# Preparation of the dense passes, kept places and the order of the plain pairs in a four-layer fp32 kernel

## The chip, the cores and the metric

The kernel runs on one core of a Trainium2 chip. A core has a matrix engine (TensorE, PE in the profile, with its weight loads as PEld), a vector engine (VectorE, DVE), an activation engine (ScalarE, ACT), a general engine (GpSimd, POOL) and a queue that issues all DMAs here (SyncE, SP). The metric is device time in microseconds; a kernel's time is the median of its runs. All arithmetic is in fp32, so each product on TensorE is recorded as two matmul instructions.

## The reference, cut to what matters

The input x is 2 x 1024 x 1024 (two batches of 1024 rows, 1024 columns). Four layers with a residual each follow one another:

```python
x = x + attn_a(layernorm(x))     # 32 heads of 32, causal, rotary, plus 10 adapter keys
x = x + ffn(layernorm(x))        # first dense pass
x = x + attn_b(layernorm(x))     # 8 heads of 16, not causal, with biases
x = x + ffn(layernorm(x))        # second dense pass, the same weights

def ffn(x):
    base = x @ W_base.T + b_base                       # 1024 x 1024
    weights = sparsemax(x @ W_router.T + b_router)     # over 8 experts
    h = einsum('bsd,edr->bser', x, lora_A)             # rank 16 each
    return base + einsum('bser,bse,ero->bso', h, weights, lora_B)
```

So a dense pass is, for each row, one large product, and a low-rank part: a hidden vector of 8 x 16 values, scaled by the router's weights, times lora_B.

## The kernel before

**Attention and filler.** `attend` runs an attention in rounds. In a round it issues the score products of one piece twice, in the two layouts (`st` at L394 for the output, `sc` at L322 for the row maximum), the exponential of `st` on ScalarE (`pt`, L506), the row minimum of the negated scores on VectorE (L335, into `part` and `nmax`), the exponential of those for the sums (`pr`, L343), and the output products (`y`, L416). Between the rounds, TensorE is given other work, the filler, by `fill.run`: so many estimated nanoseconds of it. For attention B that is 2650 a round in the first half and 1500 in the second (`FILL_B`). TensorE's order is written by hand this way, SP's too after attention A; VectorE, ScalarE and GpSimd get their order from the framework's scheduler, and every engine works through its order without overtaking.

**Filler as generators.** The filler is a queue of Python generators in `Filler`. A generator yields after each product a number of nanoseconds, or a mark. `WAIT` ends the round's filler. `AHEAD` makes the Filler call `prepare` on the next `Dense` in the queue, if its gate is open; one such call runs that generator to its next mark, and `READY` says that it is prepared. When a gate opens later, `fill.open` makes up for the calls missed. When a `Dense` that isn't ready comes to the front of the queue inside an attention, `step` prepares it once and gives the round no filler; outside (`cold`), it prepares it to the end and goes on at once. `fill.need` runs filler until a key is there.

From attention B on the queue is: first pass of batch 0 (`f1(0)`), projection of B for batch 0 (`project_b(0)`), `f1(1)`, `project_b(1)`, and then, behind gates, the second pass in four ranges of four 128-row tiles (`f2`), each opened by the output projection (`project_wo`) of the rows that it needs. Attention B of batch 0 starts behind `project_b(0)`, that of batch 1 behind `project_b(1)`.

**A dense pass** (`ffn`) works on pairs of tiles, the odd one first (`seq`). `fetch` loads a tile of x, `normalize` is the layer norm (L244 to L261) followed by the addition of the bias on GpSimd (L239), `turn` transposes the normalized tile on TensorE (L204, into a bank of PSUM, copied out by L232 or L234), `hidden` makes the low-rank hidden values and the router's logits (`hp`) and runs the router on VectorE (L1221 to L1243, which ends with the scaled hidden values `hs`), `turned` transposes these (`ht`) and copies them out on ScalarE (`hwT`, L1266). Ahead of the first pair a pass calls `fetch(0)` and `fetch(1)`, `normalize(0)` and `normalize(1)` in that order, with marks between them.

Most pairs use a scheme with seven products of half-size blocks instead of eight (`seven_added`), with sums of blocks as factors. It needs *places*: a ring for the summed weights, which `piece` loads from `tf` in DRAM, a work tile, and a third tile cut into a place for one x (`room["x"]`) and one transposed tile (`room["xt"]`). They are the tiles in which attention B keeps its q, k and v. `take_room` asks for them, in each `ffn` anew, so that each new set has to wait for the tile before it as a whole.

Two first pairs are done plainly (`plain`): that of the very first pass, where the summed weights are only being made, and that of the first second-pass range (`late_room`), where attention B still has the places. A plain pair is 2 tiles by 2 column halves (n) by 8 products `fo` of 128 x 512, each group closed by the low-rank product with `hwT` and by an addition on VectorE (L1318). In the first pass's pair n=0 goes wholly ahead of n=1, and `turned` comes right ahead of the first low-rank product, after eight products; in the `late_room` pair four products of n=0 come first, then n=1, then the rest of n=0, and `turned` comes after twelve.

PSUM banks: `bank` is one bank, shared by the output projection, the low-rank transpose and some others; `next_bank` goes back and forth between two, so that a bank comes back after one group.

**The projection of B** (`project_b`) goes tile by tile, t = 0 to 7: v (`bv`), then the transposes of the next tile, its layer norm two tiles ahead, then q and k (`bq`), which VectorE shuffles into two layouts (L1489 to L1494). It gives `AHEAD` at the head of tiles 6 and 7.

**The output projection** (`project_wo`) is called in the attention's `late` hook, one product `bo` a round. It loads x (`xo`), adds the bias on GpSimd, and starts with the round in which the attention's output `yT` is copied out by ScalarE (L1545).

The second-pass range of tiles 4 to 7 of batch 0 has a case of its own, `behind`:

```python
behind = (b, k, tiles[0]) == (0, 1, 4)
fetch(0)
if not behind:
    fetch(1)
...
if behind:
    fetch(1)
    yield WAIT
    yield WAIT
    normalize(1)
    yield WAIT
```

Of the kernel before, what the change touches and what calls it, by code (L numbers as in the profile page):

```python
# [14 lines left out]
F32 = mybir.dt.float32  # L15
# [5 lines left out]
P = 128  # L21
B, T, C = 2, 1024, 1024
NT = T // P
# [124 lines left out]
def tile_model(ctx: ExitStack, tc: tile.TileContext, d, out: bass.AP):  # L148
# [1025 lines left out]

    tf = {(i, c): dram.tile([P, HF], F32, name=f"tf{i}_{c}") for i in (2, 3, 4) for c in range(4)}

    def ffn(b, k, src, dst, w, wk, tiles, places, free=lambda: True, there=lambda t: True):


# [4 lines left out]

        seq = [t for p in range(0, len(tiles), 2) for t in (tiles[p + 1], tiles[p])]
        xs, xns, xts, hws, stores = {}, {}, {}, {}, deque()
        room = {}

        def fetch(i):
            t = seq[i]  # L1190
            xs[t] = room["x"] if room and i % 4 == 3 else wk.tile([P, C], F32, tag="x", name=f"xf{b}_{k}_{t}", bufs=3)
            sp.dma_start(xs[t], src(t))

        def normalize(i):
# [90 lines left out]

        def plain(p):
            order = [(n, c) for n in range(2) for c in range(NC)]
            if late_room:
                order = order[:4] + order[NC:] + order[4:NC]
            for i in range(2):  # L1290
                t = seq[2 * p + i]
                ops = {}
                for n, c in order:
                    cols = slice(n * HF, (n + 1) * HF)
                    if n not in ops:
                        ops[n] = next_bank([P, HF], f"fo_f{b}_{k}_{t}_{n}")
                    op = ops[n]
                    mm(op, lhsT=xts[t][:, c, :], rhs=w["wb"][:, c, cols], start=(c == 0), stop=False)
                    yield HF * COL
                    if late_room and (n, c) == (0, 3):  # L1300

                        pin_add(xs[t][:, HF:], op, xs[t][:, HF:])
                    if (i, n, c) == (0, 0, 3):
                        normalize(2)
                    if late_room and (i, n, c) == (1, 0, 1):
                        while stores:
                            sp.dma_start(*stores.popleft())
                        fetch(3)
                    if (i, n, c) == ((1, 1, 5) if late_room else (0, 1, 3)):
                        normalize(3)  # L1310
                    if i and c == 5:
                        yield from turn(2, (1 - n if late_room else n,))
                    if c < NC - 1:
                        continue
                    if (i, n) == (0, int(late_room)):
                        hwT = turned(p)
                    mm(op, lhsT=hwT[:, 1 - i], rhs=w["lb"][:, cols], start=False, stop=True)
                    dve.tensor_add(xs[t][:, cols], op, xs[t][:, cols])  # L1318
                    store(t, n)
                    yield HF * COL  # L1320
            yield from transposed(xns[seq[3]], place_xt(3), f"f{b}_{k}_{seq[3]}", by=(next_bank, next_bank))
            fill.flush("wb")
            if first:
                b11, b12 = (w["wb"][:, :4, n * HF : (n + 1) * HF] for n in range(2))
                for c in range(4):
                    fill.chore("wb1", lambda c=c: pin_sub(b12[:, c], b12[:, c], b11[:, c]))

        def take_room():
            ring, work, more = places()
            room.update(ring=ring, work=work, x=more[:, :2].rearrange("p a c -> p (a c)"),  # L1330
                        xt=more[:, 2:].rearrange("p a (b c) -> p (a b) c", c=P))
            if not first:
                for c in range(4):
                    piece(2, c)


        behind = (b, k, tiles[0]) == (0, 1, 4)
        fetch(0)
        if not behind:
            fetch(1)  # L1340
        yield None
        normalize(0)
        if not behind:
            yield None
            normalize(1)
        yield READY
        if not late_room:
            take_room()
        if behind:
            fetch(1)  # L1350
            yield WAIT
            yield WAIT
            normalize(1)
            yield WAIT
        for i in range(2):
            yield from turn(i, by=(bank, next_bank))
        n_pairs = len(tiles) // 2
# [77 lines left out]
    def project_b(b, w, fk, wk, st):  # L1435
        xs, ready = {}, {}

        def fetch(t):
            xs[t] = fk.tile([P, C], F32, tag="x", name=f"xb{b}_{t}", bufs=3)
            sp.dma_start(xs[t], x2[b, t])  # L1440

        def normalize(t):
            xn = layernorm(fk, "xn", xs.pop(t), f"b{b}_{t}", behind=True)
            ready[t] = xn, fk.tile([P, NC, P], F32, tag="xt", name=f"xt_b{b}_{t}", bufs=2)

        fetch(0)
        fetch(1)
        yield None
        normalize(0)
        yield READY  # L1450
        qk = st["qk", b] = wk.tile([P, 2, T], F32, tag=f"qkb{b}", name=f"qk{b}", bufs=1)
        kq = st["kq", b] = wk.tile([P, 2, T], F32, tag=f"kqb{b}", name=f"kq{b}", bufs=1)

        vm = st["vm", b] = wk.tile([P, NT, HB, 2 * EB], F32, tag=f"vm{b}", name=f"vm{b}", bufs=1)
        pool.memset(vm, 0.0)
        normalize(1)
        fetch(2)
        fetch(3)
        yield from transposed(*ready[0], f"b{b}_0", by=(bank, next_bank))
        for t in range(NT):  # L1460
            xnT = ready.pop(t)[1]
            if t >= NT - 2:
                yield AHEAD
            cols = slice(t * P, (t + 1) * P)
            vp = next_bank([P, P], f"bv{b}_{t}")
            for c in range(NC):
                mm(vp, lhsT=xnT[:, c, :], rhs=w["wv"][:, c, :], start=(c == 0), stop=(c == NC - 1))
                yield P * COL
            for s in range(2):
                hs, cs = slice(4 * s, 4 * s + 4), slice(s * EB, (s + 1) * EB)  # L1470
                o = slice(4 * s * EB, (4 * s + 4) * EB)
                dve.tensor_add(
                    vm[:, t, hs, cs], vp[:, o].rearrange("p (h e) -> p h e", e=EB),
                    w["b_v"][:, o].rearrange("p (h e) -> p h e", e=EB),
                )
            if t + 1 < NT:
                yield from transposed(*ready[t + 1], f"b{b}_{t + 1}", by=(bank, next_bank))
            if t + 2 < NT:
                normalize(t + 2)
            if t + 4 < NT:  # L1480
                fetch(t + 4)
            qp = next_bank([P, 2, P], f"bq{b}_{t}")
            for j in range(2):
                for c in range(NC):
                    mm(qp[:, j, :], lhsT=w["wqk"][:, c, j * P : (j + 1) * P], rhs=xnT[:, c, :],
                              start=(c == 0), stop=(c == NC - 1))
                    yield P * COL
            both = fk.tile([P, 2, P], F32, tag="both", name=f"both{b}_{t}", bufs=1)
            dve.tensor_add(both, qp, w["b_qk"][:, :, None].to_broadcast([P, 2, P]))  # L1489
            dve.tensor_scalar(qk[:, :, cols], both, low, None, ALU.mult)  # L1490
            for j in range(2):
                dve.stream_shuffle(kq[:, j, cols], both[:, j], [(i + EB) % (2 * EB) for i in range(2 * EB)])

            dve.tensor_scalar(kq[:, :, cols], kq[:, :, cols], low, after, ALU.mult, ALU.add)  # L1494
        yield ("bproj", b)

    def project_wo(b, n, yT, w, fk):
        xs = {}

        def fetch(i):  # L1500
            xs[i] = fk.tile([P, C], F32, tag="xo", name=f"xo{b}_{4 * n + i}", bufs=2)
            sp.dma_start(xs[i], x2[b, 4 * n + i])
            pool_add(xs[i], xs[i], w["b_o"])

        fetch(0)
        fetch(1)
        yield 0.0
        for i in range(4):
            t = 4 * n + i
            x = xs.pop(i)  # L1510
            for h in range(2):
                op = bank([P, HF], f"bo{b}_{t}_{h}")
                mm(op, lhsT=yT[:, i * P : (i + 1) * P], rhs=w["wo"][:, h * HF : (h + 1) * HF], start=True, stop=True)
                dve.tensor_add(x[:, h * HF : (h + 1) * HF], op, x[:, h * HF : (h + 1) * HF])
                if h == 0:
                    yield HF * COL
            sp.dma_start(x3[b, t], x)
            fill.done.add(("x3", b, t))
            if i == 1:
                fill.open(("wo", b, n))  # L1520
            if i + 2 < 4:
                fetch(i + 2)
            yield HF * COL
# [205 lines left out]
```

## Time and profile before

| | us |
|---|---|
| median of 3 runs (2460.93 to 2471.85) | 2467.08 |
| profiled execution, its own time | 2465.06 |
| its span | 2463.3 |
| PE busy | 2375.2 (96%) |
| DVE busy | 1433.7 (58%) |
| ACT busy | 1100.7 (45%) |
| POOL busy | 593.4 (24%) |
| mean granted clock of PE over the span | 0.988 |

Attention A, its projection and the first normalizations fill the span up to about 1461 us. Then come the first pass of batch 0 (to about 1605), the projection of B for batch 0 (to about 1659), attention B with the rest as filler (from 1671 to about 2298, with the projection of batch 1 ending at about 1969), and the last two second-pass ranges without an attention beside them.

A line of the timeline names its start, its length, engine, code line, operation, output and input by the program's names, shapes and count; in brackets stands how long the engine was idle ahead of it, and what released it. A list of waits gives the engine and line that waited, what for, the total, the number of times and the longest. The row "PEclk" and the last-but-two column of a table by stretches give the clock that TensorE was granted, 1.00 being full speed. A matmul row's end is modelled and lies about 0.2 us behind the start of the next matmul.

### The profile page before, as it was taken

The numbers are of one execution on the slowest core, as the hardware profiler recorded it, in microseconds if no ns is written. First come the engines' busy times: TensorE is split into PE (matmuls) and PEld (weight loads), VectorE is DVE, ScalarE is ACT, GpSimd is POOL, SyncE is SP. The second block draws the span as 40 slices with busy tenths as digits, with TensorE's granted clock in tenths as the row PEclk, the third lists the DMA queues.
The fourth block names the chain that finished last, engine by engine and source line by source line (L and its number), as shares of the span: only waits on it lengthen the run. The fifth ranks groups of instructions, "written<-read, shape, count | busy, mean of one in ns | idle before, by whom it ended". The sixth has DMA issues, their size and how long they took to land.

```text
span 2463.3 us, 60412 instructions
## 1 busy us (share of the span) xinstructions
PE 2375.2 (96%) x25063; PEld 1089.1 (44%) x25063; DVE 1433.7 (58%) x4310; ACT 1100.7 (45%) x2104; POOL 593.4 (24%) x927
## 2 busy tenths in 40 slices
PE   7999999999999999999999999999999989989999
PEld 4435444455344545444433444584334633223354
DVE  7676665666656666665631254476656756563444
ACT  2246665665665666656642000012454445654100
POOL 1332232232423322332211132202111102121332
PEclk9999999999999999999999999999999999989999
DMA  6633332323333333323212754432332202122443
GB/s 216 208 93 88 99 92 79 104 88 104 124 97 105 89 108 98 89 83 125 87 58 89 240 176 133 150 112 86 95 95 87 96 18 95 56 107 95 168 156 120
DMA packets 173043, 271.54 MB, mean 110 GB/s; under 512 B 16224, under 2 KB 76768, under 8 KB 172768
## 3 DMA queue, kind: packets, MB, share of 16 engines
q1 hardware_dynamic: 172768, 267.68, 33.8%
q8 instruction: 196, 3.21, 0.5%
q14 instruction: 79, 0.65, 0.1%
HBM read 212.05 MB, written 55.57 MB: 109 GB/s over the span
## 4 chain that ended last, share of the span: by engine, by line
PE 84%; DVE 8%; DMA 3%; ACT 2%; issue 1%; POOL 1%; SPq 1%; DVEq 0%; POOLq 0%
PE st L394 9%; PE sc L322 8%; PE y_A L416 5%; PE y L200 5%; PE z L200 3%; PE st L392 3%; PE y_f L198 3%; PE z_f L198 3%; PE x L200 3%; PE y_v L200 3%; PE y_f L200 2%; PE x_f L198 2%; PE y_B L416 2%; PE y_p L198 2%; DVE pr_A L335 2%; PE x_v L200 2%
## 5 line engine op out<-in xcount | busy, mean ns | idle before, releaser
L506 ACT ACTIVATE pt<-st 128x1024 f32<-128x1024 f32 (+1 forms) x418 | 426.0, 1019 | 617.9 <-PE st L394 483.6
L343 ACT ACTIVATE pr_A<-pr_A,nmax_A 128x896 f32<-128x896 f32 (+7 forms) x512 | 389.9, 765 | 53.3 <-DVE nmax_A L335 52.9
L335 DVE CUSTOM_DVE_ANT_0 pr_A<-sc,mask 128x512 f32<-128x512 f32 (+3 forms) x512 | 250.9, 537 | 193.7 <-PE st L394 99.4
L322 PE MATMUL sc<-kT,qT 32*128 32x512 f32 (+3 forms) x1536 | 326.3, 521 | 4.1 <-POOL qT L816 2.1
L394 PE MATMUL st<-qT,kT 32*128 32x512 f32 (+3 forms) x1536 | 306.2, 485 | 0.0
L335 DVE CUSTOM_DVE_ANT_0 pr_A<-sc,mask,part_A 128x512 f32<-128x512 f32 (+1 forms) x256 | 156.2, 647 | 146.6 <-PE sc L322 96.3
L401 POOL TENSOR_SCALAR_AFFINE_SELECT pt<-pt 128x256 f32<-128x256 f32 x256 | 105.2, 429 | 466.1 <-ACT pt L506 466.1
L343 ACT ACTIVATE pr_B<-pr_B,nmax_B 128x1024 f32<-128x1024 f32 x128 | 145.5, 1139 | 49.4 <-DVE nmax_B L335 49.3
L239 POOL TENSOR_TENSOR xf<-xf,b_base 128x256 f32<-128x256 f32 x100 | 73.1, 763 | 390.1 <-DVE xn_f L261 347.7
L416 PE MATMUL y_A<-pt,v 128*32 128x512 f32 (+3 forms) x1536 | 157.0, 496 | 0.0
L322 PE MATMUL sc<-kq,qk 32*128 32x512 f32 x512 | 147.3, 652 | 7.1 <-DVE nmax_B L335 4.8
L394 PE MATMUL st<-rows_B,kq 32*128 32x512 f32 x512 | 145.2, 643 | 6.4 <-ACT pt L506 6.0
L394 PEld LDWEIGHTS st<-qT,kT 32*128 32x128 f32 x1536 | 133.5, 185 | 16.4 <-issue 11.4
L392 PE MATMUL st<-rows_A,ones 3*128 3x512 bf16 (+3 forms) x768 | 127.6, 329 | 4.0 <-DVE nmax_A L335 3.5
L335 DVE CUSTOM_DVE_ANT_0 pr_B<-sc,zeros,part_B 128x512 f32<-128x512 f32 x128 | 90.9, 747 | 63.9 <-PE sc L322 63.9
L335 DVE CUSTOM_DVE_ANT_0 pr_B<-sc,zeros 128x512 f32<-128x512 f32 x128 | 83.4, 687 | 74.7 <-PE sc L322 74.7
L392 PEld LDWEIGHTS <-ones 3*128 3x128 bf16 x768 | 36.6, 91 | 193.3 <-issue 185.9
L322 PEld LDWEIGHTS sc<-kT,qT 32*128 32x128 f32 x1536 | 112.9, 184 | 18.0 <-issue 4.7
L815 POOL TENSOR_TENSOR qr<-qr,sin 128x256 f32<-128x256 f32 x64 | 60.5, 946 | 227.7 <-DVE qr L811 226.8
L343 ACT ACTIVATION_READ_ACCUMULATOR pr_A<-pr_A,nmax_A 128x1 f32 x512 | 97.1, 190 | 0.0
L200 PE MATMUL y<-tt,wqk 128*32 128x512 f32 x768 | 92.6, 594 | 0.0
L416 PEld LDWEIGHTS y_A<-pt,v 128*32 128x32 f32 x1536 | 33.6, 108 | 117.8 <-issue 108.0
(427 smaller groups left out, 4235.1 us busy)
## 6 DMA issues: line engine op xcount, KB each, us to landing
tt<-td SPq DMA_DIRECT2D x252, 256.0 KB, 2.8
qkb_f<-tf SPq DMA_DIRECT2D x84, 256.0 KB, 2.9
qkb_s<-tf SPq DMA_DIRECT2D x84, 256.0 KB, 3.1
wqk<-in_w_attnT SPq DMA_DIRECT2D x32, 512.0 KB, 5.1
xf<-x SPq DMA_DIRECT2D x25, 512.0 KB, 4.0
xa<-in_x SPq DMA_DIRECT2D x16, 512.0 KB, 6.0
wv<-in_w_attnT SPq DMA_DIRECT2D x8, 1024.0 KB, 5.4
yd<-ys SPq DMA_DIRECT2D x32, 256.0 KB, 2.5
```

Source lines behind the costliest of these rows:

```text
L198: return pe.matmul(out, lhsT=lhsT, rhs=rhs, start=start, stop=stop, skip_group_check=True)
L200: pe.matmul(out[i : i + 32], lhsT=lhsT[:, i : i + 32], rhs=rhs, start=start, stop=stop, skip_group_check=True)
L239: pool.tensor_add(dst[:, i : i + 2 * P], a[:, i : i + 2 * P], b[:, i : i + 2 * P])
L322: yield w * COL, lambda: pe.matmul(dst[:, o : o + w], lhsT=self.qt[rows, qc : qc + P], rhs=self.kt[rows, c0 : c0 + w], start=True, stop=True)
L335: minimum[0] = dve.tensor_tensor_reduce(pr[:, c0 : c0 + w], sc[:, i, o : o + w], m, -self.scale, BIG if c0 == 0 else self.part[:, col], AL ...
L343: tc.keep_in_program_order(act.activation(pr[:, :nk], pr[:, :nk], AF.Exp, bias=self.nmax[:, col], scale=-1.0, accum_out=self.sums[:, col]))
L392: yield w * COL / 4, lambda: pe.matmul(dst[:, o : o + w], lhsT=of["ones"][three, :], rhs=self.rows[three, off : off + w], start=True, stop ...
L394: yield w * COL, lambda: pe.matmul(dst[:, o : o + w], lhsT=self.kt[rows, kb * P : (kb + 1) * P], rhs=rhs, start=self.extra, stop=True)
L401: pool.affine_select(out=dg, in_=dg, compare_op=ALU.is_ge, fill=0.0, base=0, pattern=[[0, 2], [1, P]], channel_multiplier=-1)
L416: pe.matmul(self.y[32 * h : 32 * h + 32, off : off + w], lhsT=self.value(h, kb), rhs=pt[h // 2][:, h % 2, o : o + w], start=self.opens, st ...
L506: act.activation(pt[:, :, low_:wide_], st[:, :, low_:wide_], AF.Exp, scale=ts[0][0].scale)
L815: pool.tensor_mul(qr[:, hs], qr[:, hs], sin[:, cols][:, hs])
```

## The change

There are five edits, all in the order of the work; no product is added or left out.

1. `project_b` gives a third `AHEAD`, behind the v products of tile 6. The pass behind it is thereby prepared in three goes: both fetches at the head of tile 6, the first normalization behind tile 6's v, the second at the head of tile 7.
2. The places are kept in a dictionary outside `ffn`: one for each batch's first pass, and one for all four second-pass ranges. `take_room` asks for places only if none are there. In the second pass the tile that goes to `room["x"]` is now the range's second (i % 4 == 1), if the places are there already, instead of its fourth.
3. The case `behind` is gone; tiles 4 to 7 start like any other range.
4. Both plain pairs take the same order: four products of n=0, eight of n=1, four of n=0. `turned` comes after ten products, and the first low-rank product after twelve.
5. `project_wo` yields once more ahead of its first product, which so moves by one round.

```diff
+    kept = [{}, {}, {}]
+
     def ffn(b, k, src, dst, w, wk, tiles, places, ...):
-        room = {}
+        room = kept[2 if k else b]
         def fetch(i):
             t = seq[i]
-            xs[t] = room["x"] if room and i % 4 == 3 else wk.tile(...)
+            xs[t] = room["x"] if room and i % 4 == (1 if k else 3) else wk.tile(...)
         def plain(p):
             order = [(n, c) for n in range(2) for c in range(NC)]
-            if late_room:
-                order = order[:4] + order[NC:] + order[4:NC]
+            order = order[:4] + order[NC:] + order[4:NC]
...
                     if i and c == 5:
-                        yield from turn(2, (1 - n if late_room else n,))
+                        yield from turn(2, (1 - n,))
+                    if (i, n, c) == (0, 1, 5):
+                        hwT = turned(p)
                     if c < NC - 1:
                         continue
-                    if (i, n) == (0, int(late_room)):
-                        hwT = turned(p)
         def take_room():
-            ring, work, more = places()
-            room.update(...)
+            if not room:
+                ring, work, more = places()
+                room.update(...)
             if not first:
                 for c in range(4):
                     piece(2, c)
-        behind = (b, k, tiles[0]) == (0, 1, 4)
         fetch(0)
-        if not behind:
-            fetch(1)
+        fetch(1)
         yield None
         normalize(0)
-        if not behind:
-            yield None
-            normalize(1)
+        yield None
+        normalize(1)
         yield READY
         if not late_room:
             take_room()
-        if behind:
-            fetch(1)
-            yield WAIT
-            yield WAIT
-            normalize(1)
-            yield WAIT
...
     def project_b(...):
             if t >= NT - 2:
                 yield AHEAD
...
+            if t == NT - 2:
+                yield AHEAD
             if t + 1 < NT:
                 yield from transposed(...)
...
     def project_wo(...):
         fetch(0)
         fetch(1)
         yield 0.0
+        yield 0.0
```

## The prediction

> **What bounds the kernel now.** I read the page's first two parts, then TensorE's waits, its rows in order of time from 1450 us on (attention A, before that, is untouched), and the granted clock in short stretches.
>
> ```profile
> span 2463.3 us, 60412 instructions
> PE 2375.2 (96%) x25063; PEld 1089.1 (44%) x25063; DVE 1433.7 (58%) x4310; ACT 1100.7 (45%) x2104; POOL 593.4 (24%) x927
> PEclk9999999999999999999999999999999999989999
> ```
>
> TensorE is busy for 96%, so the kernel can win only what TensorE stands still (88 us in all), and what it runs at half clock. The waits (total, times, longest) name the few that this change touches:
>
> ```profile
> PE xt_f L204 <- DVE xn_f L261: 15.4, 3, 5.8
> PE st L394 <- ACT pt L506: 6.0, 10, 2.0
> PE ht_f L204 <- DVE hs_f L1243: 3.8, 3, 3.3
> PE bo L200 <- ACT yT L1545: 2.8, 4, 0.7
> PE fo_f L198 <- ACT hwT_f L1266: 2.7, 2, 2.3
> ```
>
> In order of time (start, length, what, in brackets the idle time before it):
>
> ```profile
> 1477.38 0.44 PE L204 MATMUL ht_f<-ident,hs_f 128*128 128x128 f32 x2 [3.29 <-DVE hs_f L1243]
> 1478.28 1.55 PE L198 MATMUL fo_f<-lb,hwT_f 128*128 128x512 f32 x2 [0.46 <-ACT hwT_f L1266]
> ...
> 1665.08 1.94 PE L204 MATMUL xt_f<-ident,xn_f 128*128 128x128 f32 x8 [5.83 <-DVE xn_f L261]
> ...
> 1974.66 1.94 PE L204 MATMUL xt_f<-ident,xn_f 128*128 128x128 f32 x8 [5.34 <-DVE xn_f L261]
> ...
> 2008.90 1.13 PE L198 MATMUL fo_f<-lb,hwT_f 128*128 128x512 f32 x2 [2.26 <-ACT hwT_f L1266]
> ...
> 2160.26 0.70 PE L394 MATMUL st<-rows_B,kq 32*128 32x512 f32 x2 [2.03 <-ACT pt L506]
> 2169.23 1.94 PE L204 MATMUL xt_f<-ident,xn_f 128*128 128x128 f32 x8 [4.19 <-DVE xn_f L261]
> ```
>
> These are six places: the first plain pair (1477), the start of the dense pass behind each projection of B (1665, 1974), the second plain pair (2009), the start of the second-pass range of tiles 4 to 7 (2150 to 2170), and the output projections (four waits of 0.70). A stall costs more than its length (stretch, its length, busy us of PE, PEld, DVE, ACT, POOL, then the granted clock and DMA):
>
> ```profile
> 1478.00:1480.00 2.00, 1.72 (x3) 0.93 (x4) 1.25 (x3) 0.23 (x1) 0.00 (x0) 0.71 0.72 262
> 1480.00:1482.00 2.00, 2.00 (x3) 0.67 (x2) 1.97 (x4) 0.00 (x0) 0.00 (x0) 0.50 0.36 132
> ...
> 1666.00:1668.00 2.00, 2.00 (x11) 2.00 (x10) 1.18 (x2) 0.59 (x1) 2.00 (x3) 0.50 0.02 4
> 1668.00:1670.00 2.00, 2.00 (x11) 2.00 (x11) 0.32 (x1) 0.00 (x0) 0.31 (x1) 0.50 0.03 8
> 1670.00:1672.00 2.00, 2.00 (x15) 1.41 (x14) 0.00 (x0) 0.00 (x0) 0.00 (x0) 1.00 0.00 0
> ```
>
> After the stall TensorE works at half clock for some 3.5 to 6 us, and loses half of that.
>
> **The change part by part.** No product is added or removed; all of it is order.
>
> *First plain pair.* Four products take 3.44 us (1510.21 to 1513.65), 0.86 each. The transpose of the low-rank input is now asked for after ten products, not eight: 1.72 us later. What it waits for, hs, ends at 1477.3 and stays there: in the built order one batch-norm statistic (0.68) of the earlier-called fourth normalization takes the place ahead of it of one weight sum (0.68), and its input landed at 1467.7 (issued 1463.0, 4.7 to land). So the stall goes from 3.29 to 1.57, and the copy hwT (0.37) lies beside two products: 0.46 gone. Half clock here cost (0.29+0.50+0.06) x 2 us = 1.70 (1482 to 1484 has 0.94). Against this the new order hands the bank of n=0 straight to the next tile: its first product waits for the addition L1318 (starts 0.04 after the matmul row's end, 0.69 long, release 0.17; the row's end is 0.2 after the next issue): 1.1 us, and the same behind the pair, where a wait of 0.42 stood: 0.7. 1.72+0.46+1.70-1.8 = **2.1** (0.4 if the clock still drops; 3.9 without the bank waits).
>
> *Third go behind the projections (1665 and 1974).* The second tile's normalization was called only when TensorE needed it:
>
> ```profile
> 1653.05 0.42 DVE L1489 TENSOR_TENSOR both<-bq,b_qk 128x256 f32<-128x256 f32 x1 [2.88 <-PE bq L198]
> ...
> 1660.87 0.68 DVE L244 BATCH_NORM_STATS2 stats_f<-xf 128x6 f32<-128x512 f32 x1
> ...
> 1664.12 0.81 DVE L261 TENSOR_SCALAR xn_f<-xf,mv_f,r_f 128x1024 f32<-128x1024 f32 x1
> ```
>
> It is two statistics, five tiny operations and L261: about 3.2 us of VectorE (0.68+0.63+0.20+0.13+0.27+0.15+0.21+0.81=3.1), two 0.20 activations, four GpSimd additions of 0.73, and, for the first pass, take_room's four DMAs on SP (already issued without a wait at 1641). Now the first tile's chain falls into VectorE's hole of 2.88 us before 1653, the second's behind the sixth tile's kq, ending by my count at 1657.9; wanted at 1659.25. Both inputs are there (fetched by 1641, 4 us to land), and the statistic of the third tile, which the order puts inside the chain, reads data issued at 1647.2 and 1957.3, early enough. What is late next: the copies out of the bank (0.24 us, as at the same transposes elsewhere), and GpSimd. Its additions now lie beside VectorE's work on the last qk. [...] I take 0.4 in the queue, 0.3 on TensorE. Gains: 5.83 + 0.5 x (1670.0-1665.1) = 8.3, less 0.3, **8.0**; 5.34 + 2.97 (half clock 1974.7 to 1979.0, 0.60 until 1981) - 0.3 = **8.0**. Each between 5 and 8.3.
>
> *Second plain pair.* The order stays; only the transpose comes two products earlier. The copy hwT then stands before one pt and two pr exponentials on ScalarE instead of behind them; they (and through them VectorE's next minima) wait 0.37 us more. **2.2** of 2.26 (1.5 at worst).
>
> *Places handed on, tiles 4 to 7.* Before, this range fetched its second tile late (issued 2157.3, into a buffer of the running pair), gave away three filler turns, and normalized then. TensorE idled 1.17+0.63+2.03+4.19 = 8.02 us between 2153 and 2170, and the clock cost 1.70 (2161 to 2165) and 2.96 (2169 to 2176). Now the fetch goes into the place kept (unused so far), the normalization is called at the end of product 4, and three bare rounds get 1.3 us of filler each. Not all comes back: ScalarE needs about 3.2 us a round there (bare rounds started 3.16 apart), the round becomes about 4.05, and VectorE's L257 waits for ScalarE's Exp, with the next minima queued behind it. I leave 2.5 us standing: 12.7-2.5 = **10.2** (6 to 12.7). On SP this fetch stands ahead of one xo load and one store; it waits for nothing.
>
> *One empty turn before the output projection.* Three waits of 0.70 in attention go: 2.1. At the end (0.70, 0.87 and 1.81 from 2298 to 2315) the last two projections now fall among the next range's transposes and share their bank: I count 0.6 + 1.3 + 0.1. 3.4-2.0 = 1.4. **3.5** (-1 to 5).
>
> [...]
>
> Sum: 2.1+8.0+8.0+2.2+10.2+3.5 = 34.0. The rounds of attention B are dealt anew, and there waits of 1 to 2.2 us cost 1.7 to 3.4 us of clock each (2025 to 2035, 2083 to 2090, 2200 to 2210): one such more, net, 3. So **31 us**. The profiled execution took 2465.1, span 2463.3 plus 1.8 around it, 2.0 below the median of three; I expect a span near 2432 and a median of 2467-31 = **2436**.
>
> **Rivals.** *(1) Half.* VectorE is just the next in line: the copies and the router keep TensorE waiting 3 us at 1665 and 1974, the clock still falls, and bare rounds stay ScalarE's. Then 2+5+5+2+5+1 = 20 less 3: 2450. For it: VectorE is busy 4.2 of 5 us there. Against it: it has holes of 2.9 us in both.
>
> *(2) Cover is missing and it is no change.* If VectorE's L257, waiting for ScalarE, holds up the minima at every moved normalization in attention, three times 5 us and a clock drop of 2.5 are new, 22; 2467-34+22 = 2455.
>
> *(3) Slower: thin filler keeps the clock down.* In the last 60 rounds (2065 to 2298) a round has only 0.9 to 1.7 us of filler. If the re-dealt rounds each leave about a microsecond open, the clock falls again and again, at 1.7 to 3.4 us each. At 2.5 each some 14 drops eat the gain; 18 give 2478. Before there were four in these rounds, and the filler between is nearly the same, so it is unlikely.
>
> **How the numbers follow.** The case as summed, 2424 to 2446: 0.67. Half, 2446 to 2454: 0.18. No change: 0.10. Slower: 0.05. 0.5% is 12 us, about what this kernel's runs (2460.9 to 2471.9) can tell from nothing. Faster 0.85, same 0.10, slower 0.05. The parts' bounds added, with 3 us of re-dealt rounds either way, give 14 to 43 us; the range they make, 2424 to 2453, leaves out some 2 in 10.
>
> **What would show it.** Right: no xt_f wait on xn_f above 1 us; a clock of 1.00 at the starts behind both projections; ht_f's first wait near 1.6 us with fo_f and xt_f waiting about 1 us on L1318; no bo wait on yT; filler in the three bare rounds. Wrong: xt_f still waiting on xn_f, longer waits of sc on nmax_B or part_B, or new rows of 0.5 clock between 2065 and 2310.

## The result and the profile after

The changed kernel takes 2444.65 us, the median of four runs (2442.70 to 2446.86), against 2469.47 us for the kernel before in four runs beside it. The ratio is 0.991, 95% interval 0.9891 to 0.9929: by the ratio 22 us faster, between 17 and 27, by the medians 24.8. Run once more later beside other kernels it took 2444.33 us, ratio 0.9897 (0.9877 to 0.9917). Forecast were 2436 us and a range of 2424 to 2453. So the direction and the range were right, and 31 us were some 6 to 9 us too many.

First the head of the changed kernel's page:

```profile
span 2445.2 us, 60552 instructions
PE 2374.2 (97%) x25135; PEld 1084.3 (44%) x25135; DVE 1434.9 (59%) x4310; ACT 1100.3 (45%) x2104; POOL 591.3 (24%) x927
```

TensorE's busy time is nearly what it was (2374.2 against 2375.2 us), so 17.1 of the 18.1 us by which the span is shorter came out of its idle time. The 72 further matmuls are no further products: among attention's rounds a product of the filler is issued in four strips, eight instructions instead of two, and twelve more products fall there than before. Its waits after the change (total, times, longest), as far as they answer to those of before:

```profile
PE sc L322 <- DVE nmax_B L335: 10.0, 7, 2.8
PE sc L322 <- DVE part_B L335: 5.6, 4, 3.5
PE ht_f L204 <- DVE hs_f L1245: 2.2, 2, 2.0
PE xt_f L204 <- ACT xt_f L234: 1.5, 5, 0.6
PE fo_f L198 <- DVE xf L1319: 0.8, 1, 0.8
PE xt_f L204 <- DVE xf L1319: 0.8, 1, 0.8
```

The 15.4 us of xt_f on xn_f, the 2.7 us of fo_f on hwT_f and the 2.8 us of bo on yT are gone. In their place the scores (sc) wait for VectorE's minima: 15.6 us, where the kernel before had 6.9:

```profile
PE sc L322 <- DVE nmax_B L335: 4.8, 4, 2.2
PE sc L322 <- DVE part_B L335: 2.1, 2, 1.0
```

In order of time, in the changed kernel:

```profile
1481.26 0.44 PE L204 MATMUL ht_f<-ident,hs_f 128*128 128x128 f32 x2 [1.98 <-DVE hs_f L1245]
...
1663.07 1.09 PE L204 MATMUL xt_f<-ident,xn_f 128*128 128x128 f32 x8 [0.24 <-ACT xt_f L234]
...
1967.97 1.09 PE L204 MATMUL xt_f<-ident,xn_f 128*128 128x128 f32 x8 [0.24 <-ACT xt_f L234]
...
2017.16 1.35 PE L322 MATMUL sc<-kq,qk 32*128 32x512 f32 x4 [2.42 <-DVE nmax_B L335]
...
2157.38 1.62 PE L322 MATMUL sc<-kq,qk 32*128 32x512 f32 x4 [3.50 <-DVE part_B L335]
...
2168.27 2.08 PE L322 MATMUL sc<-kq,qk 32*128 32x512 f32 x4 [1.58 <-DVE nmax_B L335]
```

Behind both projections the start is now clean (0.24 instead of 5.83 and 5.34). The last three rows are where the gain went: in the second plain pair's rounds, and in just those rounds of tiles 4 to 7 that the change was to fill. What VectorE did while TensorE stood before 2157.38, by its own timeline:

```profile
2150.42 0.69 DVE L224 TENSOR_TENSOR kqb_s<-kqb_s,xt_f 128x512 f32<-128x512 f32 x1
2155.42 0.69 DVE L244 BATCH_NORM_STATS2 stats_f<-xf 128x6 f32<-128x512 f32 x1 [4.31 <-DMA xf<-x]
2156.03 0.67 DVE L335 CUSTOM_DVE_ANT_0 pr_B<-sc,zeros 128x512 f32<-128x512 f32 x1
```

It stood still too, for 4.31 us, with a batch-norm statistic at the head of its queue whose input (tile 7) was still in transfer, issued only at 2148.60. The minimum that TensorE waited for was ready to run and stood behind it. In the built order this is the statistic of the second half of tile 7's columns: the kernel keeps only the first half's statistic in program order, and the second half's goes where the scheduler puts it. The clock in those stretches (same columns as in the prediction):

```profile
1665.00:1670.00 5.00, 5.00 (x64) 3.57 (x66) 3.09 (x9) 0.00 (x0) 0.16 (x1) 1.00 0.02 3
...
2155.00:2160.00 5.00, 2.62 (x12) 0.70 (x16) 2.96 (x9) 0.00 (x0) 1.98 (x3) 0.79 0.36 147
2160.00:2165.00 5.00, 5.00 (x78) 2.22 (x68) 3.68 (x17) 0.51 (x1) 4.01 (x6) 0.87 0.01 3
2165.00:2170.00 5.00, 3.31 (x16) 0.80 (x8) 3.15 (x18) 2.93 (x6) 0.00 (x0) 0.81 0.00 2
2170.00:2175.00 5.00, 5.00 (x26) 0.99 (x24) 1.43 (x4) 3.23 (x5) 0.00 (x0) 0.51 0.00 0
```

Two theories came out of this. *Queue:* the parts are worth about what was counted, but the order in which VectorE is handed its work takes a part of it back: statistics that wait for transfers, and behind them the router's chain of small instructions, ahead of the minima. *Size:* the parts were counted too high, and other waits would fill these rounds in any case. The experiments undo the parts one at a time, then mend VectorE's order with and without the change. All were timed in five rounds against the kernel before, on three chips, on which that kernel took 2467.4 to 2468.7 us.

In the traces I compare the starts of the same products. They can be compared only from the first hp_f product of the dense passes on (L198): up to there all these kernels do the same work, and yet it started between 1463.1 and 1470.2 us. Differences of up to seven microseconds between two spans thus arise ahead of anything that the edits touch.

### The profile page after: what moved, and what is told of

The parts are those of the page before. It is cut to its first block, busy times and chain, and to the rows that moved or that the text cites. A ratio compares the mean times of both kernels' runs of the same rounds, so it can differ in the third digit from the quotient of the medians.

```text
span 2445.2 us, 60552 instructions
## 1 busy us (share of the span) xinstructions
PE 2374.2 (97%) x25135; PEld 1084.3 (44%) x25135; DVE 1434.9 (59%) x4310; ACT 1100.3 (45%) x2104; POOL 591.3 (24%) x927
## 4 chain that ended last, share of the span: by engine, by line
PE 84%; DVE 9%; DMA 2%; ACT 2%; issue 1%; POOL 1%; SPq 1%; DVEq 0%; POOLq 0%
PE st L394 9%; PE sc L322 8%; PE y_A L416 5%; PE y L200 5%; PE y_f L198 4%; PE z L200 3%; PE st L392 3%; PE z_f L198 3%; PE x L200 3%; PE y_v L200 3%; PE x_f L198 2%; PE y_B L416 2%; PE y_f L200 2%; PE y_p L198 2%; DVE pr_A L335 2%; PE x_v L200 2%
## 5 line engine op out<-in xcount | busy, mean ns | idle before, releaser
L239 POOL TENSOR_TENSOR xf<-xf,b_base 128x256 f32<-128x256 f32 x100 | 73.0, 760 | 378.2 <-DVE xn_f L261 328.7
L322 PE MATMUL sc<-kq,qk 32*128 32x512 f32 x512 | 146.9, 650 | 15.6 <-DVE nmax_B L335 10.0
```

The source lines that it names most:

```text
L239: pool.tensor_add(dst[:, i : i + 2 * P], a[:, i : i + 2 * P], b[:, i : i + 2 * P])
L322: yield w * COL, lambda: pe.matmul(dst[:, o : o + w], lhsT=self.qt[rows, qc : qc + P], rhs=self.kt[rows, c0 : c0 + w], start=True, stop=True)
```

## Experiments: undoing the parts

**The third go behind the projections.**

```diff
-            if t == NT - 2:
-                yield AHEAD
```

> The changed kernel with the third go behind attention B's projections taken out again, nothing else. Theory (third go worth what the two traces show, 7.3 us at the first projection and 7.75 at the second): 15 us slower than the changed kernel, ratio to the kernel before 0.997 instead of 0.991, about 2460 us where the kernel before has 2468; waits of xt_f on xn_f of 5 to 6 us at both places with half clock behind them. Rival (half: VectorE is just the next in line): 8 to 10 us slower, ratio 0.9945.

Measured: 2457.08 us, ratio 0.9963 (0.995 to 0.9976), 12.4 us slower than the changed kernel. Both old waits are back, to the hundredth:

```profile
1666.67 1.94 PE L204 MATMUL xt_f<-ident,xn_f 128*128 128x128 f32 x8 [5.83 <-DVE xn_f L261]
...
1977.40 1.94 PE L204 MATMUL xt_f<-ident,xn_f 128*128 128x128 f32 x8 [5.34 <-DVE xn_f L261]
```

Against the changed kernel the lag grows by 8.1 us at the first place (from -1.98 to +6.10 us) and by 7.6 us at the second (+4.32 to +11.95). The rounds between give some 4 us back (6.1 to 4.3, later 11.9 to 9.8), which is why the times show 12.4 and not 15.7. The prediction's two times 8.0 stand; the rival "half" falls.

**The empty turn before the output projections.**

```diff
         fetch(1)
         yield 0.0
-        yield 0.0
```

> The changed kernel with one empty turn before the output projection, as it was before. Theory of the prediction (the turn is worth 3.5 us): ratio 0.9925, four waits of bo on yT of about 0.7 us back. Theory from the two traces (the turn earns 3.4 us at the end, but in the first output projection of attention the rounds dealt anew cost 2 us more): ratio 0.9915, the end 3.4 us longer and attention's rounds 34 to 43 about 2 us shorter. Rival (the turn is what costs the rounds, all along): ratio 0.990 or below.

Measured: 2449.02 us, ratio 0.993 (0.9915 to 0.9946), 4.4 us slower; predicted were 3.5. The waits of bo on yT are back:

```profile
PE bo L200 <- ACT yT L1541: 2.8, 4, 0.7
```

But the trace deals the sum differently: without the extra turn attention's rounds were 3.6 us *better* (the lead grew from 3.36 us before the first projection to 6.96 us at the last second-pass pair in attention) and the end was 5.0 us worse (6.96 to 1.97). It still ends ahead because the profiled execution, 2444.90 us, is the shortest of this kernel's six. If both were real, the turn belongs to the last projection alone, which the next run tried:

```diff
         fetch(1)
-        yield 0.0
+        if (b, n) == (1, 1): yield 0.0
         yield 0.0
```

> The changed kernel with the second empty turn only ahead of the last output projection (second image, second half); the other three have one turn, as before. Theory from the run with one turn throughout (its trace: 3.6 us better in attention, 5.0 us worse at the end): both are had, 3 to 4 us faster than the changed kernel, ratio 0.9895. Rival (the 3.6 us were chance of the rounds' clock, and three waits of 0.7 us come back): 0 to 2 us slower, ratio 0.9915.

Measured: 2444.07 us, ratio 0.9912 (0.9897 to 0.9928): no change. My theory fell, the rival held. The 3.6 us did not repeat and so pass for the luck of re-dealt rounds; in attention the three turns are worth nothing that shows, though they do remove three waits of 0.7 us, and the whole gain lies at the end, where the prediction had put the smaller half.

**The first plain pair in its old order.**

```diff
-            order = order[:4] + order[NC:] + order[4:NC]
+            if late_room:
+                order = order[:4] + order[NC:] + order[4:NC]
...
-                        yield from turn(2, (1 - n,))
-                    if (i, n, c) == (0, 1, 5):
+                        yield from turn(2, (1 - n if late_room else n,))
+                    if late_room and (i, n, c) == (0, 1, 5):
                         hwT = turned(p)
...
+                    if not late_room and (i, n) == (0, 0):
+                        hwT = turned(p)
```

> The changed kernel with the first plain pair in its old order (both halves of the tile's columns one behind the other, the transpose of the low-rank input behind eight products); the second plain pair stays. Theory from the two traces: worth 0.2 us, so within 1 us of the changed kernel (ratio 0.991), with the waits of 3.3 and 0.46 us back and the two bank waits of 0.78 us gone. Rival (the prediction's 2.1 us): ratio 0.992, about 2 us slower from 1480 us on.

Measured: 2444.00 us, ratio 0.9914 (0.9897 to 0.993): the part is worth nothing that can be timed. The old wait came back, longer than before:

```profile
1485.34 0.69 PE L204 MATMUL ht_f<-ident,hs_f 128*128 128x128 f32 x2 [4.42 <-DVE hs_f L1245]
```

From that first hp_f product to the second pair's ht_f the old order took 54.18, 55.77 and 54.30 us in three traces, the new one 54.00 in the changed kernel and between 51.7 and 54.4 in the six others that have it and VectorE's order as it was.

**The places handed on.** Undone by giving each second-pass range its own places again, with the late fetch and the three WAITs as they stood before (the diff of the change, backwards, in ffn, fetch and take_room).

> The changed kernel with the places not handed on: each second-pass range takes its own again, and the range of tiles 4 to 7 fetches its second tile late, gives three filler turns away and normalizes then, as before. Everything else stays changed. Theory from the two traces (handing on brought 3.7 us, since it uncovered a wait of 3.5 us and left the clock low): 3.5 to 4.5 us slower than the changed kernel, ratio to the kernel before 0.9927, the wait of xt_f on xn_f of about 4 us back. Rival (the prediction's 10.2 us): ratio 0.995.

Measured: 2441.31 us, ratio 0.9898 (0.9881 to 0.9915). Both expectations were wrong in sign: without this part the kernel is 3.3 us *faster* by the medians, not to be told from no difference by the intervals, and certainly not 10.2 us slower. In the trace of this run the old waits are back, the longest being

```profile
2149.05 1.94 PE L204 MATMUL xt_f<-ident,xn_f 128*128 128x128 f32 x8 [3.92 <-DVE xn_f L261]
```

with 1.17, 0.64 and 2.02 us of waits on ScalarE before it and a clock of 0.50 behind it, and still the changed kernel gains only 0.8 us on it from 2105 us to the end (a lag of 9.29 us there, 8.45 us at the last pair). What this run is ahead by in the trace it gains before that: 5.5 us from the first hp_f product to 2105 us, 2.3 of them in the first plain pair, which this part doesn't touch. So in its own rounds handing on the places costs about as much as it takes away; whether it costs it in VectorE's queue is what the next section tests.

**The changed kernel once more**, as a measure of all this.

> The changed kernel itself once more, unaltered, to stand beside the others on one chip: ratio 0.991 as before if the runs repeat, within 0.0015 of it.

Measured: 2444.33 us, ratio 0.9897 (0.9877 to 0.9917). The median repeats to 0.3 us; the two ratios differ by 0.0013, and each lies within the other's interval. Differences between the variants below are therefore given by medians, with ratios beside them, and under 3 us they are not read at all. This trace also shows what the first plain pair hangs on. The stretches are cut where the clock changes (the last section says how they were found); the changed kernel first, then the same kernel again:

```profile
1478.63:1482.04 3.41, 1.43 (x6) 0.55 (x5) 3.41 (x8) 0.31 (x1) 1.76 (x2) 1.00 0.41 154
1482.04:1485.46 3.42, 3.42 (x6) 1.36 (x5) 2.82 (x9) 0.47 (x3) 0.00 (x0) 0.50 0.64 232
```

```profile
1475.93:1479.35 3.42, 2.56 (x6) 0.78 (x5) 3.42 (x9) 0.00 (x0) 2.74 (x4) 1.00 0.02 8
1479.35:1482.76 3.41, 1.49 (x5) 0.85 (x6) 3.41 (x8) 0.37 (x1) 1.05 (x1) 1.00 0.41 154
1482.76:1486.17 3.41, 3.41 (x9) 1.52 (x8) 3.38 (x9) 0.41 (x2) 0.00 (x0) 1.00 0.83 306
```

TensorE stood 1.98 us in the first and 2.78 us in the second, and it was the shorter wait that cost the clock. From the first hp_f to the second pair's ht_f it took 54.00 and 52.71 us: a gain of 0.2 or of 1.5 us over the 54.18 of before. The waits differ because a statistic on VectorE, which stands ahead of hs, waited for its transfer, again the changed kernel first:

```profile
1470.22 0.69 DVE L244 BATCH_NORM_STATS2 stats_f<-xf 128x6 f32<-128x512 f32 x1 [0.51 <-DMA xf<-x]
```

```profile
1470.22 0.69 DVE L244 BATCH_NORM_STATS2 stats_f<-xf 128x6 f32<-128x512 f32 x1 [1.30 <-DMA xf<-x]
```

## Experiments: mending VectorE's order

**Tile 7's statistic alone.** The second half's statistic of this one normalization is kept behind the first half's. No product, transfer or copy moves; on VectorE the statistic goes from ahead of eight minima and a router's chain to behind them.

```diff
-            if i == 0 and behind:
+            if (i == 0 or behind == 2) and behind:
                 tc.keep_in_program_order(r)
...
-            xns[t] = layernorm(wk, "xn", xs[t], f"f{b}_{k}_{t}", behind=True)
+            xns[t] = layernorm(wk, "xn", xs[t], f"f{b}_{k}_{t}", behind=2 if (b, k, t) == (0, 1, 7) else True)
```

> The changed kernel with one batch-norm statistic (second half of tile 7, first image, second pass) kept behind the first half's, so that VectorE does not come to it before its transfer has landed. Theory (this statistic, waiting 4.3 us for its transfer ahead of the minima, is why handing on the places gave 3.7 us and not 10.2): TensorE's wait of 3.5 us on part_B at 2157 us goes, and most of the low clock from 2155 to 2170 us (0.79, 0.87, 0.81): 5 to 7 us faster than the changed kernel, ratio 0.9885. Rival (the router's chain or ScalarE is next in line in the same rounds and the wait only moves): within 1.5 us of the changed kernel, ratio 0.991.

Measured: 2440.65 us, ratio 0.99 (0.9883 to 0.9917), 4.0 us faster by the medians (by the ratio, against the 0.991 and 0.9897 of the changed kernel, 2.5 us faster and none, so the time alone doesn't tell it from no change); in the trace 4.5 us at this place, from 2142 to 2190 us. Less than the theory's 5 to 7, because the rival was half right: the wait of 3.50 us is gone and the clock stays at 1.00 until 2161 us, but a few rounds on

```profile
2162.81 2.08 PE L322 MATMUL sc<-kq,qk 32*128 32x512 f32 x4 [4.16 <-DVE nmax_B L335]
```

stands where the changed kernel had 1.58: next in VectorE's line is the router, from the copy of the hidden product at 2154.55 to the last product of its weights at 2161.41, and the minima behind it.

**All the second statistics.**

```diff
-            if i == 0 and behind:
+            if behind:
                 tc.keep_in_program_order(r)
```

> The changed kernel with the second half's statistic kept behind the first half's in every normalization of the dense passes and of attention B's projections. Theory (VectorE's queue holds up the minima wherever such a statistic stands early before its transfer has landed; at 2010 to 2015 us it waits 4.66 us, and TensorE 2.42 us on nmax_B behind it, clock 0.79 and 0.87): besides the 4 us of the run that moved tile 7's statistic alone, another 3 us, 7 us faster than the changed kernel, ratio 0.988. Rival (what is in line behind it, the router's chain, takes the place): no faster than that run, ratio 0.990.

Measured: 2432.59 us, ratio 0.9863 (0.9846 to 0.988), 12 us faster than the changed kernel, more than expected. VectorE's waits for the dense passes' transfers in the changed kernel were

```profile
DVE stats_f L244 <- DMA xf<-x: 19.2, 9, 4.7
```

and in this run

```profile
DVE stats_f L244 <- DMA xf<-x: 1.1, 2, 0.7
```

TensorE's 2.42 us at 2017 us is gone, and the clock there is 1.00. The kernel before had such waits too,

```profile
DVE stats_f L244 <- DMA xf<-x: 22.1, 10, 3.9
```

yet TensorE waited only 6.9 us for the minima there. So what these waits cost went by what stood behind them, not by their length: 22.1 us of them go with 6.9 us on TensorE here, 19.2 us with 15.6 us in the changed kernel.

**The router in two pieces, too.** On top of the last run each tile's router is called one filler step later than the one before and kept behind the latest minimum.

```diff
-            dve.tensor_add(z, hp[:, P:], w["b_router"])
+            pin(dve.tensor_add(z, hp[:, P:], w["b_router"]))
...
-                router(seq[2 * p + i], hs[:, i])
+                fill.chore(('r', nm), lambda i=i: router(seq[2 * p + i], hs[:, i]))
...
-            o, e = seq[2 * p], seq[2 * p + 1]
+            o, e = seq[2 * p], seq[2 * p + 1]; fill.flush(('r', f"f{b}_{k}_{o}"))
```

> The run before this one, with the router's chain of a pair cut into its two tiles, each called one filler step later and kept behind the latest minimum. Theory (with the statistics away, the chain of 22 small VectorE instructions, 5.2 to 6.1 us, ahead of the minima is what TensorE waits for: 4.16 us on nmax_B at 2163 us in the run that moved one statistic, 2.79 us at 2073 us in the changed kernel): those two waits fall below 1.5 us and the clock behind them stays up, 5 to 7 us faster again, ratio 0.9855. Rival (the low-rank input comes later and ht_f waits for it instead, or the minima are late anyway): within 1.5 us of the run before.

Measured: 2428.09 us, ratio 0.984 (0.9824 to 0.9857), the fastest kernel of this study: 4.5 us below the run before it (expected were 5 to 7) and 16.6 below the changed kernel. Both waits the text names fell, but stay above the 1.5 us expected: that at 2073 us of the changed kernel (2.84 us in the run before this one) to 1.80 us with the clock at 1.00 behind it, the other from 4.38 us to

```profile
2148.55 2.08 PE L322 MATMUL sc<-kq,qk 32*128 32x512 f32 x4 [1.88 <-DVE nmax_B L335]
```

and behind this one the clock did not stay up:

```profile
2145.00:2150.00 5.00, 3.01 (x13) 0.80 (x8) 4.74 (x17) 2.64 (x4) 4.11 (x6) 0.84 0.00 2
2150.00:2155.00 5.00, 5.00 (x26) 0.99 (x24) 3.32 (x13) 3.52 (x7) 0.00 (x0) 0.50 0.00 0
```

**The same mendings in the kernel before.** This asks whether the change itself was worth more than it showed.

> The kernel before with the same two mendings (second statistics kept behind the first, routers cut in two and kept behind the latest minimum), none of the change. Theory (the change moved work into rounds in which VectorE's queue was badly ordered, so the mendings are worth less here than their 16 us in the changed kernel): 6 to 10 us faster than the kernel before, ratio 0.997, and the change is then worth about 30 us, near the prediction's 31. Rival (the mendings are worth the same in both, and the parts were mis-sized): 16 us faster, ratio 0.9935, and the change worth 23 us as measured.

Measured: 2460.32 us, ratio 0.9965 (0.9954 to 0.9975). The two mendings bring 8 us here (2468.70 to 2460.32) and 16.6 us in the changed kernel. So between mended kernels the change is worth 2460.3 - 2428.1 = 32.2 us, by the ratios (0.9965 - 0.984) x 2468 = 31 us, where it is worth 22 to 25 us unmended. By the ratios' intervals alone the two overlap (roughly 26 to 36 us, and 17 to 30), so the difference is likely rather than certain. The theory "queue" predicted it, "size" did not. What is left of TensorE's waits on the minima in the two mended kernels, the kernel before first:

```profile
PE sc L322 <- DVE nmax_B L335: 1.5, 2, 0.9
```

```profile
PE sc L322 <- DVE nmax_B L335: 5.1, 4, 1.9
```

**The places again, mended.** The mended changed kernel with the places not handed on.

> The kernel with statistics and routers kept behind (ratio 0.984), with the places not handed on, as in the run that undid this part alone. Theory (handing on is worth its 10.2 us once VectorE no longer holds up the minima in the rounds it uncovers; without that it was worth about nothing): 6 to 9 us slower than the mended kernel, ratio 0.987. Rival (the part was over-counted from the start, ScalarE or something else fills those rounds): 0 to 3 us slower, ratio 0.9845.

Measured: 2434.94 us, ratio 0.9857 (0.9835 to 0.9879), 6.8 us slower by the medians, 4.2 by the ratios, whose intervals overlap; 4.8 us in the trace, from 1554 us to the end, 2.4 of them ahead of the range itself. Handing on the places thus seems to bring something once the queue is mended, some 4 to 7 us with all that comes along and 2.4 in the range itself, where it brought nothing or lost 3 us before. But it doesn't come to 10.2 us, even then.

## Why the prediction was right, and where it was wrong

Most of the sum can be set against the two pairs of traces, by the starts of the same products (before minus after, us):

| stretch | predicted | before to after | mended before to mended after |
|---|---|---|---|
| first plain pair (first hp_f to the second pair's ht_f) | 2.1 | 0.2 (1.5 in the second trace) | 3.2 |
| first projection of B (1656 to 1680) | 8.0 | 7.6 | 6.4 |
| rounds up to the second projection (1680 to 1961) | in the reserve of -3 | -2.5 | +2.0 |
| second projection and second plain pair (1961 to 2045) | 8.0 + 2.2 | 9.0 | 10.8 |
| rounds up to 2105 | in the reserve | 0.1 | -0.3 |
| tiles 4 to 7, later rounds, the end | 10.2 + 3.5 | 7.5 | 9.2 |

The first column of differences lacks 0.3 us, lost at 1622 us, and then comes to 21.6. The parts singled out by a run, changed kernel against the part undone (medians): third go 12.4 (predicted 16 less what the rounds take), empty turn 4.4 (3.5), first pair -0.6 (2.1), places -3.3 (10.2).

- *Third go: right.* 8.0 and 8.0 were predicted, 8.1 and 7.6 us came back when it was undone. The second tile's chain fell into VectorE's hole as counted, and the clock is 1.00 behind both projections. GpSimd's additions beside it cost nothing that shows at the start, where the prediction allowed 0.3 us on TensorE for them. No run shows that term: in the changed kernel TensorE waits 0.24 us there, for a copy, and not for the normalization. What the rows of the kernel before show is 0.67 us for VectorE's L1490 beside GpSimd instead of 0.35, and 0.48 for L1494 instead of 0.41; in the changed kernel the same two instructions (L1485, L1489) took 0.53 and 0.96 us at the sixth tile's place, 0.64 and 0.49 at the last tile's.
- *Second plain pair: right in its own row, but the place next to it was missed.* The wait of 2.26 is gone. The statistic of a later tile, which waited 3.36 us for its transfer in the kernel before, waits 4.66 us now, and TensorE behind it 2.42 instead of 1.13.
- *Empty turn: the size right (4.4 for 3.5), its parts not.* All of it lies at the end. The three waits of 0.70 in attention are gone from the list, but removing them moved no time: the run that gave them back was as fast.
- *First plain pair: mis-sized.* The step counted 1.57 us of waiting and no half clock. The wait was 1.98 and 2.78 us, and the clock fell in one execution and not in the other. What lengthened it is the 0.51 and 1.30 us that the third tile's statistic waited for its transfer; the prediction had checked the fourth tile's only. In the run with all second statistics kept behind, this statistic happened not to wait: TensorE's wait was 1.58 us, and the stretch took 51.51 us, 2.7 less than before. The bank waits came as counted (0.78 twice for 1.1 and 0.7). The bound of 0.4 "if the clock still drops" is what the first trace shows (0.2).
- *Places handed on: the step that failed.* The text took 12.7 us away and left 2.5 us standing, for ScalarE and for VectorE's L257 waiting for it. What stood there was something else: 3.50 us behind a statistic that waits for a transfer, 1.58 us behind the router, and in the four stretches from 2155 to 2175 us a clock that costs 2.62 x 0.21 + 5 x 0.13 + 3.31 x 0.19 + 5 x 0.49 = 4.3 us. That is 9.4 of the 12.7. The prediction looked for late transfers where it moved a fetch itself (that of the second tile), and not at the next fetch of the same range, that of tile 7. It stays at its place in the program, issued at 2148.60 and landed some 6.8 us later, while the statistic that reads it was placed so early on VectorE that it was reached at 2151.1. In the start behind the projections it had asked just this ("reads data issued at 1647.2 and 1957.3, early enough"), and there it was right.
- *Reserve for re-dealt rounds: of the right size, by luck.* Three us were kept, 2.5 us went in the rounds before 1961. With VectorE mended the same rounds gain 2.0 instead. At least in part this reserve was thus no dealing of filler but the same queue: up to 1961 us the scores wait 0.85, 1.10 and 0.79 us for minima in the changed kernel, and nowhere in the fastest one.
- *Rivals.* "No change" named the right engine, but the wrong instruction: not L257 behind ScalarE, but L244 behind a transfer. "Slower" is excluded by the interval of the time. "Half" (13 to 21 us) is not, since the interval begins at 17 us; what it put forward, 5 us at each projection, is excluded by the first run.
- *Signs.* Of the signs of being wrong that the prediction named, one came true ("longer waits of sc on nmax_B or part_B"), beside nearly all the signs of being right. The range of 29 us took in the time although one part of the sum brought next to nothing.

That the mended pair gives 31 to 32 us is not proof of every number: there the first pair gives more than predicted, the first projection less, and the places still less than 10.2. In the range of tiles 4 to 7 of the fastest kernel 1.88 us of waiting and 3.01 x 0.16 + 5 x 0.50 = 3.0 us of clock remain. The rest of the difference to 10.2 was not settled.

## What to carry to other kernels

When a change makes a stretch start earlier, go through every transfer that is used in it, not only those that the change moves, and compare issue plus landing time with the new time of use: that of tile 7, issued at 2148.60 and landed some 6.8 us later, became the new wait. VectorE worked through its built order here, so its 4.31 us of waiting fell on the minimum behind the waiting statistic, and on TensorE as 3.50 us. So look in the built order for instructions fed by transfers that stand ahead of the ones that the bottleneck engine waits for; keeping them behind was worth 12 us here, half as much as the whole change (and with the routers moved as well, 8 us in the kernel before). And time a part by undoing it: a stall that vanishes from the list of waits (three times 0.70 us) need not have moved the end.

## What the hardware did that was not expected

The clock after a short idle didn't go by the length of the idle time alone. The same kernel lost it after 1.98 us and kept it at 1.00 after 2.78 us at the same place; the fastest kernel lost it after 1.88 us (0.84, then 0.50). The granted clock shows a pattern. From 1440 us to the last product every stretch of low clock in the traces of the kernel before and of the changed kernel is 3.41 or 6.83 us long, at 0.50 throughout, and within one trace all begin a whole number of 3.413 us apart: in the changed kernel at 1482.04, 1912.12, 2017.93, 2072.55, 2157.88 and 2168.12 us (126, 31, 16, 25 and 3 of them), before at 1478.84, 1663.16, 1973.77, 2028.39, 2083.00, 2161.51, 2168.33 and 2202.47 us (54, 91, 16, 16, 23, 2 and 10). Cut into such stretches, the 1.98 us all lie in one, and the next ran at 0.50; the 2.78 us are divided into 0.86 and 1.92, and the clock stayed (the rows stand with the changed kernel's second run). In other traces' first plain pairs, waits of 1.19, 1.58 and 1.74 us ahead of ht_f (the fastest kernel, the run with all second statistics, the mended one without kept places) left it at full clock, and waits of 2.72, 3.29, 3.96 and 4.42 us (the run with the turn at the last projection alone, the kernel before, the same mended, the old order) were followed by slower products (four in 3.32 us behind the 2.72, four in 1.88 us behind the 1.58). In attention's rounds 0.79 us could be enough (1908.71 to 1912.12 in the changed kernel), so idle time is not all that counts there; the rest stayed open.

So the row of one trace doesn't give the price of a stall of 2 us: in the first plain pair it was nothing, or 3.41 us at half clock, which is 1.7 us of work. From the first hp_f product to the last product the low stretches come to 44.4 us before, 27.3 after and 6.8 in the fastest kernel. TensorE was busy for 40.3 us of the first and 27.1 us of the second; half of the difference, 6.6 us, is an estimate of the clock's share in the change's 21.6 us.

Beside GpSimd some small VectorE instructions took 2.0 to 4.3 times as long, in this router those with two tiles as inputs. One multiplication over eight elements a row in the router of the fastest kernel, with GpSimd at work and then without (its additions L239 run from 2143.52 to 2149.11 us):

```profile
2143.60 0.69 DVE L1231 TENSOR_TENSOR sup_f<-zs_f,karr 128x8 f32<-128x8 f32 x1
...
2149.52 0.16 DVE L1231 TENSOR_TENSOR sup_f<-zs_f,karr 128x8 f32<-128x8 f32 x1
```

Of the others with two tiles, L1232 took 0.53 us in the first place and 0.17 in the second, L1237 0.45 and 0.23, L1245 0.74 and 0.29; of those with one, L1229 took 0.21 and 0.22, L1241 0.15 and 0.16, L1243 0.23 both times. The whole router of a tile took 4.1 us (2143.05 to 2147.16) and 3.1 us (2148.42 to 2151.55), though the second one's first instruction still fell beside GpSimd (L1223, 0.71 us against 0.17).
